# A two-layer graph transformer on one core: both layers and the first stretch in an order that a list schedule in the kernel plans

## The chip, the core and the metric

The kernel runs on one core of a Trainium2 chip. A core has TensorE (PE; matrix products into PSUM, with PEld its weight loads), VectorE (DVE), ScalarE (ACT), GpSimd (POOL, which here issues the indirect transfers) and SyncE (SP, which issues the plain ones), each with an instruction queue of its own that runs in order, and 16 DMA engines that they share. The metric is the device time of one execution in microseconds.

## What is computed

There are 6250 nodes with 128 features and a type out of 16, and 200,000 edges, sorted by destination, with a type out of 32. Two layers of this run one after the other (H = 8 heads of HS = 16):

```python
k = typed_linear(x, ntype, Wk).reshape(n, H, HS)      # q, v alike: one 128x128 matrix for each node type
kT = jnp.einsum('nhd,htdo->nhto', k, Watt)            # one 16x16 matrix for each head and edge type
vT = jnp.einsum('nhd,htdo->nhto', v, Wmsg)
kw, m = kT[src, :, etype], vT[src, :, etype]
a = jnp.einsum('ehd,ehd->eh', kw, q[dst]) * pri[:, etype].T / SQRT_D
att = edge_softmax(a, dst, n)
hag = jax.ops.segment_sum((m * att[:, :, None]).reshape(-1, H * HS), dst, num_segments=n)
h = jax.nn.silu(typed_linear(hag, ntype, Wa))
alpha = jax.nn.sigmoid(skip[ntype])[:, None]
h = layernorm(h * alpha + x * (1.0 - alpha)) * g + b
```

The result is `layernorm(x + (h @ ff_w + ff_b))`. All data are float32.

## The kernel before

**Table.** For a layer, a table in DRAM has 32 rows for each node, one for each edge type, with 128 values of kT and 128 of vT: 49 tiles of 128 nodes, 4 MiB a tile. An edge then needs one row of the table, and a tile of 128 destination nodes gets its s-th edges by one indirect gather of 128 rows (`gather`, L544). Nodes are ordered by in-degree, so that a tile has 61 to 23 such slots: 1613 gathers a layer.

**First stretch.** The edges' start positions are found by POOL's gathers and VectorE's comparisons (L218 to L256), nodes are ordered (L259 to L315; scatter of records at L309), slots are filled (`idx_all`, L329), types and x are brought into the new order (L360 to L395). Then (L519 to L531) for each group of four tiles `typed` builds k and v: for each of 16 node types VectorE masks the transposed rows (`xm`, L472) and TensorE adds a product for each of two weights (L476). For each tile `table_rows` makes 16 products of 32 rows by 512 columns (L503), four of which use the four row groups of TensorE; VectorE (L508) and ScalarE (L510) copy them from PSUM into one buffer `st` of 4 MiB, and four transfers of 1 MiB (L531) write it to the table. Each float32 product is two instructions in the profile.

**Layers.** For a layer, `free` issues gathers on POOL into a ring of 64 (layer 0) or 96 (layer 1) slots as slots come free. `attend` does a tile in pieces of up to 16 slots: q times k (L563), sum by head (L565), a softmax over the slots (L568 to L578), weights times v (L586), sum over slots (L590, L591). When a group of four tiles is done, `behind` works on it while the next group is attended: `finish` (typed products with Wa, SiLU, mix with x, norm), then in layer 0 `project_next` (typed products k, v, q, then the table rows of layer 1 tile by tile into `st`, copied by ScalarE alone, and one indirect scatter of 4 MiB a tile on POOL, L715), in layer 1 `head` (last product, norm, one indirect scatter of the output a tile, L738). Layer 0's queries are computed in `queries`, a group ahead.

**Order.** The parts that run beside `attend` are generators; `STEPS` and `REST` say how many of their steps are taken at each pause of `attend`. Engines' queues are in order, so a step written out early waits at its place and holds what is behind it.

Of the kernel before, what the change touches and what calls it, by code (L numbers as in the profile page):

```python
# [41 lines left out]
RINGS = (64, 96)  # L42
REST = 3
BINS = 64
NBLK = 512
GT = 4
FAR = float(1 << 21)
# [4 lines left out]
ROWT = True  # L52
STEPS = {("queries", 0): 9, ("queries", 1): 1, ("behind", False): 20, ("tile", False): 8,
         ("behind", True): 33, ("tile", True): 0}
# [18 lines left out]
def gnn_kernel(ctx: ExitStack, tc: tile.TileContext, x, src, dst, etype, ntype, Wk, Wq, Wv, Wa,  # L73
# [16 lines left out]
    GROUPS = [list(range(t, min(t + GT, NTILE))) for t in range(0, NTILE, GT)]  # L90
# [3 lines left out]
    assert max(profile) + 1 <= min(RINGS)  # L94
# [9 lines left out]
    qrows = dtile("qrows", [NP, P])  # L104
# [20 lines left out]
    for state in states:  # L125
        nc.sync.dma_start(
            out=state.rearrange("(t p) c -> p t c", p=P),
            in_=init[:, None, :].to_broadcast([P, NTILE, 2 * H + P]),
        )
# [14 lines left out]
    early = ctx.enter_context(ExitStack())  # L144
    tp = early.enter_context(tc.tile_pool(name="tp", bufs=1, side="right"))
# [33 lines left out]
    nc.sync.dma_start(out=csort_rows, in_=comb)  # L179
    with tc.tile_pool(name="prep_ps", bufs=1, space=bass.MemoryType.PSUM) as pps:  # L180
# [18 lines left out]
    ps = ctx.enter_context(tc.tile_pool(name="ps", bufs=1, space=bass.MemoryType.PSUM))  # L199
    wp = ctx.enter_context(tc.tile_pool(name="wp", bufs=1))  # L200
    ap = ctx.enter_context(tc.tile_pool(name="ap", bufs=2))
    masks = [ap]

    def bank(i):


        return ps.tile([P, GT * P], F32, tag=f"b{i}", name=f"b{i}")

    def load_typed(name, w, bufs=1):
        t = (wp if name == "wa" else tp).tile([P, NT, P], F32, tag=name, name=name, bufs=bufs)  # L210
        nc.sync.dma_start(out=t, in_=w.rearrange("t d o -> d t o"))
        return t


    pp = keep.enter_context(tc.tile_pool(name="prep2", bufs=1, side="right"))
    NC1 = NTILE + 1
    stage = ExitStack()
    sp = stage.enter_context(tc.tile_pool(name="search", bufs=2, side="right"))  # L218
    nid = pp.tile([P, NC1], F32, tag="nid")
    nc.gpsimd.iota(nid, pattern=[[1, NC1]], base=0, channel_multiplier=NTILE,  # L220
                   allow_small_or_imprecise_dtypes=True)
    ones_b = pp.tile([P, P], BF16, tag="ones_b")
    nc.vector.memset(ones_b, 1.0)
# [748 lines left out]
```

## Time and profile before

| | |
|---|---|
| median of 3 runs | 6803.65 us (6802.91 to 6808.02) |
| profiled execution | 6805.36 us, span 6803.6 us |
| mean granted TensorE clock | 0.639 |
| busy: PE, DVE, ACT, POOL | 2779.5, 3521.3, 913.1, 3561.3 us |
| DMA | 950.01 MB, mean 140 GB/s |

A busy share is an average over stages with different limits; the stages are told apart in the rows below. In the rows, `a <- b` names what is written and what is read; a bracket at the end of a row is the time for which the engine had stood idle, and what released it.

### The profile page before, as it was taken

Reading aid. Unit: us, or ns where it says so; the run is one execution under the profiler, and the core shown is the slowest. Engines: PE = TensorE matmul, PEld = TensorE weight load, DVE = VectorE, ACT = ScalarE, POOL = GpSimd, SP = SyncE. Lnnn points to the kernel's source line nnn. Section 1 sums busy time; section 2 is a strip of 40 time slices with the busy share of each in tenths; the row PEclk is TensorE's granted clock in tenths of the full one; section 3 lists DMA queues with packets and bytes.
Section 4 is the critical chain, followed back from the end, with each engine's and each line's share of the span. In section 5 each row is a group of like instructions: output and inputs, shape, how many; then the busy total and the mean of one; then the engine's idle time right before and its main releaser. Section 6 shows DMA issues by size and latency. Waiting matters only on the chain.

```text
span 6803.6 us, 31981 instructions
## 1 busy us (share of the span) xinstructions
PE 2779.5 (41%) x7380; PEld 1378.6 (20%) x7380; DVE 3521.3 (52%) x4748; ACT 913.1 (13%) x1713; POOL 3561.3 (52%) x3543
## 2 busy tenths in 40 slices
PE   1569999513353443644644666730110111111203
PEld 0124444201121221222222233320000000000001
DVE  5433433456566644644543644114665666567748
ACT  0123222100211111111111112220000000000001
POOL 4530000476767747436436431027777777777774
PEclk9657777656575665766766776755555555555556
DMA  6065655633545445344345333343333333333332
GB/s 165 12 238 242 253 218 216 208 104 93 179 137 192 141 141 173 109 155 148 124 159 168 129 137 136 124 165 100 106 103 101 106 108 107 106 104 106 106 105 61
DMA packets 335615, 950.01 MB, mean 140 GB/s; under 512 B 89712, under 2 KB 173164, under 8 KB 304056
## 3 DMA queue, kind: packets, MB, share of 16 engines
q0 software_dynamic: 171376, 645.92, 29.5%
q1 hardware_dynamic: 164040, 301.98, 12.5%
q14 instruction: 140, 1.15, 0.1%
q8 instruction: 59, 0.97, 0.1%
HBM read 514.82 MB, written 432.84 MB: 139 GB/s over the span
## 4 chain that ended last, share of the span: by engine, by line
issue 54%; POOL 16%; DVE 8%; DMA 3%; PE 0%; POOLq 0%; ACT 0%; DVEq 0%; SPq 0%; another core or an unknown queue 0%; ACTq 0%
POOL ring L544 15%; DVE add L590 2%; DMA ring<-table,idx_all 2%; DVE ring L586 2%; DVE xm L472 1%; DVE ring L563 1%; DVE b L565 1%; POOL table L715 0%; POOL out_dram L738 0%; PE b L476 0%; POOLq L544 0%; DMA table<-st,rec 0%; DVE den L576 0%; DMA bk<-in_L_gnn_Watt_dram 0%; DVE b L572 0%
## 5 line engine op out<-in xcount | busy, mean ns | idle before, releaser
L544 POOL DMA_INDIRECT ring<-table,idx_all x3226 | 3239.0, 1004 | 2409.3 <-issue 973.7
L563 DVE TENSOR_TENSOR ring<-ring,b 128x2048 f32<-128x2048 f32 (+13 forms) x269 | 469.6, 1749 | 1484.4 <-DMA ring<-table,idx_all 1459.3
L472 DVE SCALAR_TENSOR_TENSOR xm<-types,b 128x512 f32<-128x512 f32 (+1 forms) x1040 | 627.2, 651 | 1177.3 <-PE b L476 1090.2
L503 PE MATMUL b<-bv,vT 32*128 32x512 f32 x1568 | 740.4, 1023 | 1035.2 <-ACT st L510 975.3
L510 ACT COPY st<-b 128x512 f32<-128x512 f32 x1225 | 644.9, 593 | 1217.0 <-DMA table<-st,rec 802.4
L590 DVE TENSOR_REDUCE add<-ring 128x128 f32<-128x2048 f32 (+13 forms) x269 | 733.1, 2725 | 0.2
L503 PE MATMUL b<-bk,kT 32*128 32x512 f32 x1568 | 673.7, 987 | 119.5 <-ACT st L510 117.1
L503 PEld LDWEIGHTS b<-bv,vT 32*128 32x128 f32 x1568 | 313.2, 278 | 1276.6 <-ACT st L510 1131.5
L476 PE MATMUL b<-xm,wk 128*128 128x512 f32 (+1 forms) x832 | 456.0, 633 | 240.5 <-DVE xm L472 238.0
L463 PE MATMUL b<-ident,hag 128*128 128x128 f32 x98 | 28.8, 374 | 1259.2 <-DVE hag L835 1116.4
L476 PE MATMUL b<-xm,wq 128*128 128x512 f32 (+1 forms) x832 | 433.1, 644 | 159.9 <-DVE xm L472 145.9
L565 DVE TENSOR_REDUCE b<-ring 128x128 f32<-128x2048 f32 (+13 forms) x269 | 470.8, 1750 | 0.6
L586 DVE TENSOR_TENSOR ring<-ring,b 128x2048 f32<-128x2048 f32 (+13 forms) x269 | 462.9, 1744 | 0.0
L476 PE MATMUL b<-xm,wv 128*128 128x512 f32 (+1 forms) x832 | 441.4, 615 | 0.0
L508 DVE COPY st<-b 128x512 f32<-128x512 f32 x343 | 225.5, 688 | 412.6 <-DMA table<-st 207.9
L476 PE MATMUL b<-xm,wa 128*128 128x512 f32 (+1 forms) x832 | 398.0, 635 | 100.1 <-DVE xm L472 100.1
L503 PEld LDWEIGHTS b<-bk,kT 32*128 32x128 f32 x1568 | 292.7, 271 | 293.7 <-ACT st L510 215.1
L715 POOL DMA_INDIRECT table<-st,rec x49 | 49.1, 1003 | 557.0 <-ACT st L510 513.4
L573 ACT ACTIVATE b<-b 128x264 f32<-128x264 f32 (+21 forms) x98 | 37.4, 381 | 2027.1 <-DVE b L572 2010.7
L463 PEld LDWEIGHTS b<-ident,hag 128*128 128x128 f32 x98 | 15.0, 171 | 1278.0 <-DVE hag L835 1124.6
L476 PEld LDWEIGHTS b<-xm,wk 128*128 128x128 f32 x832 | 168.1, 212 | 445.5 <-DVE xm L472 270.8
L476 PEld LDWEIGHTS b<-xm,wq 128*128 128x128 f32 x832 | 176.1, 221 | 396.0 <-issue 200.5
(155 smaller groups left out, 1873.0 us busy)
## 6 DMA issues: line engine op xcount, KB each, us to landing
table<-st SPq DMA_DIRECT2D x196, 1024.0 KB
ring<-table,idx_all POOLq DMA_INDIRECT x3226, 2.8
types<-tyrow SPq DMA_DIRECT2D x36, 256.0 KB
state<-init SPq DMA_DIRECT2D x2, 3528.0 KB
state<-state SPq DMA_DIRECT2D x98, 72.0 KB
xs<-xperm SPq DMA_DIRECT2D x24, 256.0 KB
rows<-in_x_dram SPq DMA_DIRECT2D x12, 256.0 KB
types_i<-in_node_type_dram SPq DMA_DIRECT2D x12, 256.0 KB
```

Source lines behind the costliest of these rows:

```text
L463: nc.tensor.transpose(t_ps[:, j * P : (j + 1) * P], rows[:, j], ident)
L472: nc.vector.scalar_tensor_tensor(xm[:, i, :M], types[:, :M], float(t0 + i), xT[:, :M], op0=ALU.is_equal, op1=ALU.mult)
L476: nc.tensor.matmul(acc[c][:, :M], w[:, t0 + i], xm[:, i, :M], start=(t0 + i == 0), stop=(t0 + i == NT - 1))
L503: nc.tensor.matmul(tab, cT[c][rows, nodes], blk[rows, t0 : t0 + per].rearrange("p t o -> p (t o)"), start=True, stop=True)
L508: nc.vector.tensor_copy(to, tab.rearrange("p (t o) -> p t o", o=width))
L510: nc.scalar.copy(to, tab.rearrange("p (t o) -> p t o", o=width))
L544: nc.gpsimd.indirect_dma_start(out=rings[-1][:, place], out_offset=None, in_=tables[layer], in_offset=bass.IndirectOffsetOnAxis(ap=idx[:, ...
L563: nc.vector.tensor_tensor(kk, kk, q[:, None, :].to_broadcast([P, m, P]), op=ALU.mult)
L565: nc.vector.tensor_reduce(sc[:, s0 : s0 + m], kk.rearrange("p s (h d) -> p s h d", h=H), axis=AX.X, op=ALU.add)
L586: nc.vector.tensor_tensor(vv.rearrange("p s (h d) -> p s h d", h=H), vv.rearrange("p s (h d) -> p s h d", h=H), sc[:, s0 : s0 + m, :, None ...
L590: nc.vector.tensor_reduce(add, vv.rearrange("p s c -> p c s"), axis=AX.X, op=ALU.add)
L715: s = nc.gpsimd.indirect_dma_start(out=by_node, out_offset=bass.IndirectOffsetOnAxis(ap=rec[:, t0 + j, 2:3], axis=0), in_=st.rearrange("p ...
```

## The change

Nearly all of the kernel's body is written anew. What it does:

- Every part is a generator that yields what its next step needs: the engine (or two to choose from), an estimated duration, and times to wait for. `Plan.run` starts, again and again, the step that could start first by these estimates (`RANK` breaks ties) and so writes out the instructions in the order of that simulated time, inside `tc.manual_schedule()`. TensorE's steps are timed by `Clock`, whose rate goes between 1200 and 2400 columns a microsecond.
- First stretch: `prepare` (edges, order, slots) is one thread, `first_typed` and `first_tables` are others, beside it. Groups have two tiles; k and v are 256 columns wide each in one bank, and layer 0's q is computed here as well, as 128-wide products with the masked rows as weights, kept in `qall` and scattered to DRAM by position (`first_queries`). There are four banks for table products; either of ScalarE and VectorE copies them. `st` is freed by halves.
- Weights of layer 0 and the states' initial values are loaded ahead of the sort check; weights now come before the states.
- Layers: gathers, attention and what is behind are threads. `behind` holds a lock for its PSUM banks until the queries are copied, `next_tables` one for `st`. Table copies go to ScalarE or VectorE. A table scatter is placed `MARGIN` = 8 us after its planned readiness, an output scatter `LATE` = 40 us. The last groups have 3, 2, 2, 1 and 1 tiles. Rings are 64 and 96 slots, as before, allocated for each layer. q comes from DRAM in both layers and is copied into PSUM.

```diff
+MARGIN = 8.0
+RECS_US = 3.3
+XG_US = 2.4
+LATE = 40.0
+RANK = dict(table=0, empty=0, gather=1, attend=1, prepare=2, mask=3, typed=3, late=4, query=1)
+GATHER_US = 1.31
+HOP_US = 0.12
...
+    def run(self):
+        while self.threads:
+            best = None
+            for t in self.threads:
+                at = self.start(t)
+                if at is not None:
+                    key = (at[1], -1 if at[2] == "POOL" and t[0] != RANK["gather"] else t[0], t[1])
+                    if best is None or key < best[0]:
+                        best = (key, t, at)
+            _, t, (end, us, e) = best
+            if e == "PE":
+                self.free[e], end, state = self.clock.run(us, t[4][1])
+            else:
+                self.free[e] = end
+            end += HOP_US
+            self.step(t, (end, e) if isinstance(t[4][0], tuple) else end)
...
+    LAST, a = [], 0
+    for n in [GT] * ((NTILE - 9) // GT) + [GT - 1] * ((NTILE - 9) % GT // 3) + [3, 2, 2, 1, 1]:
+        LAST.append(list(range(a, a + n)))
+        a += n
...
+        plan.spawn(mask(), RANK["mask"])
+        for t in range(NT):
+            busy[t].us = yield "PE", Work(M * (len(cols) + len(rows))), [ready[t], clear]
+            xm = masks.pop(t)
+            todo = [(w, acc[:, :M], None) for w, acc in cols]
+            todo += [(w, acc[:, c : c + P], slice(c, c + P)) for w, acc in rows for c in range(0, M, P)]
+            for i, (w, to, c) in enumerate(todo):
+                last_of = t == NT - 1 and i in ends
+                if c is None:
+                    nc.tensor.matmul(to, w[:, t], xm, start=False, stop=last_of)
+                else:
+                    nc.tensor.matmul(to, xm[:, c], w[:, t], start=False, stop=last_of)
...
+                    us = yield "PE", Work(TAB, width / P), [*needs, *emptied[-len(banks):][:1]]
+                    tab = banks[len(emptied) % len(banks)]
+                    nc.tensor.matmul(tab, cT[rows, nodes], blk[rows, t0 : t0 + per].rearrange("p t o -> p (t o)"),
+                                     start=True, stop=True)
+                    def empty(to=st[:, t0 : t0 + per, c0 : c0 + width], tab=tab, done=done, us=us, i=i):
+                        done.us, e = yield ("ACT", "DVE"), (act_us(TAB), dve_us(TAB)), [us, free[i]]
+                        (nc.scalar.copy if e == "ACT" else nc.vector.tensor_copy)(
+                            to, tab.rearrange("p (t o) -> p t o", o=width))
...
+    def send(dest, c, filled, done):
+        us = yield "SP", 0.8, filled
+        for s0 in (c * RT // 2, c * RT // 2 + RT // 4):
+            nc.sync.dma_start(out=dest[:, s0 : s0 + RT // 4], in_=st[:, s0 : s0 + RT // 4])
+        done.us = (yield "DMA", 5.4, [us]) + 2.0
...
+    def first_queries():
+        for i, g in enumerate(GROUPS):
+            for t in g:
+                yield "POOL", GATHER_US, [placed, queried[i]]
+                s = nc.gpsimd.indirect_dma_start(
+                    out=qrows[0], out_offset=bass.IndirectOffsetOnAxis(ap=posn[:, t : t + 1], axis=0),
+                    in_=qall[:, t], in_offset=None, bounds_check=NP - 1, oob_is_err=False)
...
+    with tc.manual_schedule():
+        plan.spawn(first_typed(), RANK["typed"])
+        plan.spawn(first_tables(), RANK["table"])
+        plan.spawn(prepare(), RANK["prepare"])
+        plan.spawn(first_queries(), RANK["late"])
+        plan.run()
...
+    def next_tables(i, kT, vT, bk, bv, us, at):
+        turn = locks["s"].take()
+        for j, t in enumerate(LAST[i]):
+            halves = yield from table_rows(tabs, at["rows"], kT, vT, j, bk, bv, [us, turn], [at["st"]] * 2)
+            us = yield "SP", 0.0, halves[0] + halves[1]
+            us = yield "POOL", GATHER_US, [us + (MARGIN if i + 2 < NG else 0.0)]
+            s = nc.gpsimd.indirect_dma_start(
+                out=by_node, out_offset=bass.IndirectOffsetOnAxis(ap=rec[:, t, 2:3], axis=0),
+                in_=at["rows"].rearrange("p t c -> p (t c)"), in_offset=None, bounds_check=NP - 1, oob_is_err=False)
+            at["st"] = us + 16.0
+        locks["s"].give(us - MARGIN)
...
+    def gathers(layer, ring, size, landed, freed):
+        for s in range(SLOTS):
+            us = yield "POOL", GATHER_US, [freed[s - size]] if s >= size else []
+            gather(layer, ring, idx_all, s, s % size)
+            landed[s].us = us + 2.5
...
+            with tc.manual_schedule():
+                plan.spawn(gathers(layer, ring, size, landed, freed), RANK["gather"])
+                plan.spawn(attends(fp, layer, ring, cut(size), st, weights, wa, landed, freed), RANK["attend"])
+                plan.run()
```

## Rows read from the trace of the kernel before

**Rows 1.** Windows by stage: the stretch (us from the span's start), its length, busy time and (number of instructions) of PE, PEld, DVE, ACT and POOL, mean granted TensorE clock, DMA share, GB/s.
```profile
0.00:359.00 359.00, 110.64 (x410) 46.43 (x410) 164.95 (x286) 22.05 (x40) 185.91 (x181) 0.83 0.35 87
359.00:1239.00 880.00, 772.17 (x2269) 368.94 (x2269) 344.48 (x523) 249.47 (x461) 38.59 (x39) 0.74 0.60 243
...
4115.60:4538.50 422.90, 283.56 (x845) 164.52 (x845) 81.56 (x177) 119.05 (x230) 12.64 (x14) 0.69 0.38 148
1252.00:4538.50 3286.50, 1600.60 (x3958) 814.46 (x3958) 1617.97 (x2097) 526.00 (x1012) 1666.39 (x1663) 0.66 0.43 143
4538.50:6722.00 2183.50, 266.71 (x656) 132.02 (x656) 1328.95 (x1700) 102.87 (x178) 1660.38 (x1652) 0.55 0.36 105
6722.00:6803.60 81.60, 29.41 (x87) 16.76 (x87) 64.76 (x142) 12.68 (x23) 10.04 (x10) 0.65 0.06 19
```

**Rows 2.** Who reads and writes the tables: line, engine, operation, tiles and count; duration in ns (least, median, most); first and last start in us.
```profile
L544 POOL DMA_INDIRECT ring<-table,idx_all x3226: 995/1002/1686, 1252.0 to 6722.1; - x190
L531 SPq DMA_DIRECT2D table<-st x196: 319/423/2391, 359.2 to 1238.9; - x196
L715 POOL DMA_INDIRECT table<-st,rec x49: 962/1017/1018, 1754.2 to 4521.8; - x49
```

**Rows 3.** POOL's timeline around the first table scatter of layer 0: start, duration, line, operation, count, idle time before it and its releaser. Between the second and third row no other scatter is issued; the rows left out are gathers.
```profile
1754.19 1.02 POOL L715 DMA_INDIRECT table<-st,rec  x1 [0.31 <-issue]
...
1763.38 1.00 POOL L544 DMA_INDIRECT ring<-table,idx_all  x1 [0.30 <-issue]
1767.96 1.00 POOL L544 DMA_INDIRECT ring<-table,idx_all  x1 [3.58 <-DMA table<-st,rec]
```

**Rows 4.** POOL's waits: what waited for what, us in total, times, longest. The first three rows are of layer 0 (1252 to 4538.5), the fourth of 2040 to 4115, the fifth of 1250 to 2040.
```profile
POOL table L715 <- ACT st L510: 513.4, 20, 87.4
...
POOL ring L544 <- DVE add L590: 463.4, 19, 53.9
POOL ring L544 <- DMA table<-st,rec: 80.9, 22, 5.4
...
POOL table L715 <- ACT st L510: 154.0, 9, 21.5
...
POOL ring L544 <- DVE add L590: 56.4, 7, 19.1
```

**Rows 5.** Timeline of the first stretch's preparation: SP's issue of the states' initial values, the first transposes, the first gather of the edge search, the first x gather, and the copy into `st` that waited longest.
```profile
3.08 11.50 SPq L126 DMA_DIRECT2D state<-init  x2
...
72.94 1.09 PE L463 MATMUL b<-ident,rows 128*128 128x128 f32 x4
...
74.23 1.19 POOL L247 DMA_INDIRECT part<-dsort,blk_i  x1 [4.71 <-DVE blk_i L241]
...
345.58 1.00 POOL L392 DMA_INDIRECT xg<-in_x_dram,rec  x1 [0.30 <-issue]
...
370.73 1.29 DVE L508 COPY st<-b 128x512 f32<-128x512 f32 x2 [57.80 <-DMA table<-st]
```

**Rows 6.** One group of four tiles in the table stage: windows of its typed products (706 to 731) and of its table rows (731 to 775), then rows of its timeline (`x2`, `x8`: that many instructions).
```profile
706.00:731.00 25.00, 25.00 (x59) 10.92 (x59) 8.14 (x13) 0.00 (x0) 0.00 (x0) 0.99 0.13 51
731.00:775.00 44.00, 34.95 (x135) 17.20 (x133) 18.14 (x28) 20.53 (x38) 0.00 (x0) 0.80 0.81 334
...
731.94 1.14 PE L503 MATMUL b<-bk,kT 32*128 32x512 f32 x8
...
743.46 1.56 ACT L510 COPY st<-b 128x512 f32<-128x512 f32 x3 [4.12 <-DMA table<-st]
```

**Rows 7.** TensorE and ScalarE on layer 0's last tile, one tile wide: 128-wide typed products, then a single table product (two instructions) and the transpose behind it, with the copy of that transpose's operand.
```profile
4505.21 0.39 PE L476 MATMUL b<-xm,wk 128*128 128x128 f32 x2
4505.43 0.39 PE L476 MATMUL b<-xm,wv 128*128 128x128 f32 x2
...
4509.99 1.12 PE L503 MATMUL b<-bk,kT 32*128 32x512 f32 x2
4510.10 0.27 ACT L516 COPY qT<-b 128x128 f32<-128x128 f32 x1
4511.04 0.33 PE L606 MATMUL b<-ident,qT 128*128 128x128 f32 x1
```

**Rows 8.** Groups of instructions by line over the span: busy us, mean ns, idle before and releasers.
```profile
L510 ACT COPY st<-b 128x512 f32<-128x512 f32 x1225 | 644.9, 593 | 1217.0 <-DMA table<-st,rec 802.4 <-PE b L503 240.4 <-DMA table<-st 173.2
L472 DVE SCALAR_TENSOR_TENSOR xm<-types,b 128x512 f32<-128x512 f32 (+1 forms) x1040 | 627.2, 651 | 1177.3 <-PE b L476 1090.2 <-PE b L463 86.9
L508 DVE COPY st<-b 128x512 f32<-128x512 f32 x343 | 225.5, 688 | 412.6 <-DMA table<-st 207.9 <-PE b L503 204.5
```

**Rows 9.** Timeline behind layer 0's last gather: table scatters and the copies between them, the steps of `finish` from its copied product to the next typed product, the last scatter and layer 1's first gather.
```profile
4138.09 0.99 POOL L715 DMA_INDIRECT table<-st,rec  x1 [21.47 <-ACT st L510]
4149.98 2.05 ACT L510 COPY st<-b 128x512 f32<-128x512 f32 x4 [12.17 <-DMA table<-st,rec]
...
4204.78 0.59 ACT L516 COPY vT<-b 128x512 f32<-128x512 f32 x1 [15.36 <-PE b L476]
...
4216.54 2.47 DVE L472 SCALAR_TENSOR_TENSOR xm<-types,b 128x512 f32<-128x512 f32 x4
...
4521.75 0.97 POOL L715 DMA_INDIRECT table<-st,rec  x1 [35.10 <-ACTq L613]
...
4538.50 1.05 POOL L544 DMA_INDIRECT ring<-table,idx_all  x1 [15.78 <-issue]
```

More of the change, by code (lines that the diff above doesn't have):

```diff
@@ L46 @@
 GT = 4
+GL = 2
 FAR = float(1 << 21)
@@ L197, in gnn_kernel, with run @@
     prep.close()
[L199 to L211, printed above, removed]
-        return t
+    def run(steps):
+        try:
+            at = steps.send(None)
+            while True:
+                at = steps.send((0.0, at[0][0]) if isinstance(at[0], tuple) else 0.0)
+        except StopIteration as end:
+            return end.value
@@ new lines, in gnn_kernel, with apart @@
+    on_pool = [None]
+    def apart(s, group):
+        kept = [on_pool[0]] if on_pool[0] is not None else []
+        tc.declare_no_dep(s.ins, group=group, keep=kept, reason="every node has rows of its own")
+        tc.add_to_no_dep_group(group, s.ins)
+        on_pool[0] = s.ins
+    wk, wv, wq, bk, bv = w0
+    st = first.tile([P, RT, ROW], F32, tag="st", name="st")
+    made = [When() for _ in GROUPS]
+    used = [When() for _ in GROUPS]
+    columns = [None] * len(GROUPS)
+    HALF = GL * P
@@ L544, in gather @@
+    def gather(layer, ring, idx, s, place):
         nc.gpsimd.indirect_dma_start(
-            out=rings[-1][:, place], out_offset=None, in_=tables[layer],
+            out=ring[:, place], out_offset=None, in_=tables[layer],
             in_offset=bass.IndirectOffsetOnAxis(ap=idx[:, s : s + 1], axis=0),
@@ L777, in cut, with queries @@
+    def queries(rows, j, t, read, to, ready):
+        us = yield "ACT", act_us(P), [rows[1], read]
+        q = sb[:, QC:] if (profile[t] + 1) * H <= QC else ak[:, :P]
+        nc.scalar.copy(q, rows[0][:, j])
+        to[t] = q
+        ready.us = us
     def cut(size):
-        out = []
+        pieces = []
         for t in range(NTILE):
@@ L833, in gnn_kernel @@
+                _, den = yield from attend(ring, pieces[t], pen_all[:, span], profile[t], qs[t],
+                                           states[layer][t * P : (t + 1) * P], hag[:, j], landed[span], free, [ready[t]],
+                                           read[t])
+                past[t].us = plan.free["DVE"]
+                us = yield "DVE", 0.4 + dve_us(P), ()
                 nc.vector.tensor_scalar(den, den, 1e-30, None, op0=ALU.max)
```

1124 lines of the change are left out of this document (667 added, 457 removed).

## The prediction

> **What bounds the kernel now.** I read the windows by stage first, then POOL's waits, then single places of the timeline. [rows 1] cut the span of 6803.6 us at the first and last gather of each layer [rows 2]: a first stretch of 1252 us, layer 0 from 1252 to 4538.5, layer 1 from there to the end. The profiled run took 6805.4 us, its span 6803.6, the median of the runs is 6803.65: the sum below is of spans and stands for the median as it is.
>
> Layer 1 is bound by POOL. A gather starts every 1.31 us ((1763.38 - 1754.19) / 7) [rows 3], and 1613 gathers with 45 output scatters at that price are 2172 us; the stage took 2183.5 from first to last gather [rows 1]. Nothing but the 81.6 us behind the last gather can still be won there.
>
> Layer 0 issues 1613 gathers and 49 table scatters, 1662 x 1.31 = 2177 us, and takes 3286.5. The difference of 1110 us is POOL standing still, and the waits say for what [rows 4]: 513 us a table scatter waited for ScalarE's copies into st, of which 154 lie among the gathers and the rest behind the last one; 463 us a gather waited until VectorE freed ring slots; 81 us a gather waited until a table scatter had landed; some 50 us are small. No engine is full: VectorE is busy 1618 of 3286 us, TensorE 1601 [rows 1]. So layer 0 is a matter of order: VectorE and TensorE come to the projection in lumps, and POOL's queue holds scatters that are not ready.
>
> The first stretch has two parts that barely overlap. In 359 us the edges are sorted into slots, POOL going from step to step [rows 5], and the first table rows leave only then: a copy into st waited 57.8 us for the first transfer [rows 5]. Then 880 us of table, in turns: for four tiles, 30 us of typed products with TensorE full at a clock of 0.99 of 2.4 GHz and DMA at 0.13, then 44 us of table rows with DMA at 0.81 and 334 GB/s, where the copies wait for transfers [rows 6].
>
> **The change, part by part: first stretch.** It removes the turns (typed products and table rows are interleaved), hides the preparation, and adds layer 0's queries here. Per tile of 128 nodes, at the full clock: a 512-wide product is two instructions of 25.00 / 59 = 0.42 us, 0.85 [rows 6], so k and v for 256 columns cost 16 x 2 x 0.43 / 2 = 6.9 us a tile (half the columns, two tiles). The queries use 128-wide products at 0.22 us each [rows 7]: 16 x 0.22 = 3.6. A batch of four 32-row table products runs side by side, eight instructions in 1.14 us [rows 6]; a lone one holds TensorE as long, 1.05 us until the next instruction starts, whose operand was copied by 4510.4 [rows 7]. Sixteen products are then 4.6 us in full batches, 16.8 us one by one. Transposes 0.3. That is 15.4 to 27.6 us. I take 16.4, near the lower end: there are four banks, ScalarE and VectorE empty one in 0.59 and 0.69 us [rows 8], so some three or four are free whenever a typed step of 1.3 us is over.
> Transfers do not bind: 196 writes of 1 MiB [rows 2] are 205 MB, at 334 / 0.81 = 412 GB/s 499 us, and all DMA of the first 359 us is 0.35 of them, 126 us [rows 1]; together 625 of some 800.
> POOL's preparation takes 272 us from 74 to the first x gather at 346 [rows 5]: 148 instructions of 1.31 are 194, 78 are gaps. With the x gathers and the new query scatters it is 246 instructions, 322 us, and ends near 74 + 78 + 322 = 474; at twice the price an instruction, if transfers are late beside the table's, near 796. Both lie before the table's end, so I cost it at nothing; without that cover it is the 272 us again.
> The first transposes start at 73 us now; SP's state writes, 11.5 us of issue, are put ahead of them [rows 5], so I start at 85. Then 49 x 16.4 = 804, 16 us for the last transfer and the first gather: 905, where 1252 is now. Bounds: 15.4 gives 856. At the clock of 0.74 that the table stage has on average [rows 1] 16.4 becomes 22.2 and the stretch 1189; I take the full clock, because it stood at 0.99 where TensorE was kept full [rows 6] and here it hardly pauses.
>
> **Layer 0.** The list schedule moves work between queues but leaves POOL's 2177 us. What is left of the waits:
> - Table scatters: the eighth POOL transfer behind one waits until it has landed, 3.58 us [rows 3]. It showed 22 times only [rows 4], since POOL stood for other reasons at the rest. With a stream that does not stop it comes 49 times: 175 us. This is a part of today's time that the change uncovers. Bounds 81 to 175.
> - Ring: 56.4 us in the first 790 us of the layer [rows 4], where the tiles have 61 to 37 of 64 slots and little else runs. The ring is not changed, so I keep 60; bounds 0 (a plan that frees in time) and 150 (a third of today's 463).
> - Scatters that wait for st: 154 among the gathers today [rows 4]. The scatter is now placed 8 us behind its planned readiness; I take 45, bounds 0 and 154: nearer to none, since a tile's chain (30 us, below) is shorter than its gathers.
> - Behind the last gather: 423 us today [rows 1], because the last five tiles' projection runs alone, with 87 us of typed products [rows 4] and 22.4 a tile of table rows [rows 9]. The last groups are now of 3, 2, 2, 1, 1 tiles, and for one tile the chain is landing 3, attention 13 (half of the 1329 / 49 = 27 us that VectorE spends on a tile in layer 1 [rows 1], as the rest comes before the last landing), typed products 4 + 11 (48 x 0.22), the norm between them 12 (4204.8 to 4216.5) [rows 9], table copies on two engines 7, scatter to first gather 17 (4521.75 to 4538.50) [rows 9]: 67. The group ahead holds the same lock for up to one such chain without landing and scatter: 110 taken, bounds 67 and 150.
> Cover: a tile's own table chain is 11 us of copies on ScalarE alone, 1 of issue, 11.4 of transfer, 22.4 [rows 9], with the 8 us margin 30; the last tiles' gathers take 24 x 1.31 + 5 = 36 us. TensorE needs four maps of 16 products at 0.22, 14 us, and 5 for tables; at half the clock 38. VectorE has 1618 us today, loses the query masks (208 x 0.65 = 135) and gains up to half of 784 table copies (270): 1753. All below 2567, but TensorE at half clock would just fail at the end.
> Sum 2177 + 175 + 60 + 45 + 110 = 2567.
>
> **Layer 1.** 2183.5 stays; the output scatters are put 40 us late so that they do not hold gathers. Behind the last gather a single tile: 3 + 13 + 4 + 12 and 8 for the head = 40, and 15 for the tile ahead of it: 55. Together 2238.
> Total 905 + 2567 + 2238 = 5710 us, a ratio of 0.839.
>
> **The rivals.**
> A. TensorE pays for the mixing. If table products come alone between full-height ones, a tile costs 27.6 us and the first stretch 85 + 1352 + 16 = 1453: the total is 6258. For it speaks the 1.05 us of the lone product [rows 7]; against it, four banks that come free by themselves. The Trainium skill, TensorEngine Tiling (Array Packing), Key Properties, says that a change of tiling mode drains TensorE. The 1.05 us row agrees in kind; by the rule each of 16 turns a tile would pay it.
> B. Layer 0's order does not come out on the chip: POOL's 1110 us stay, of whatever names. 905 + 3286 + 2238 = 6429. The lumps would have to survive a plan that models each engine.
> C. The other side. POOL's queue is in order, and a scatter placed too early holds every gather behind it, and they hold VectorE. If TensorE lags behind the plan, each group's first scatter waits for the typed products, 87 us, and each other one 21.5, as behind the last gather today [rows 4, 9]: 15 x 87 + 34 x 21.5 = 2036 us, and 7746 in all. It decides from (6817 - 5710) / 49 = 22.6 us a scatter on. Against it: chains of 30 us under 36 to 60 us of gathers, and a late group is not early again for the next.
> D. The landing waits vanish too, since plan or ring stalls absorb them, and the order holds: 5710 - 175 - 60 - 45 = 5430.
>
> **How the numbers follow.** Forecast case 0.64, D 0.16, A 0.09 (partly, between 5900 and 6258), B 0.07, C 0.04 (half of it above 6817). The prediction is 5710. The range goes down to D's 5430 and up to 6050, where the clock of the first stretch lies at its average today (5710 + 284 = 5994) or scatters and ring take their upper bounds (5710 + 109 + 90 + 40 = 5949); beyond it lie B, C and half of A, and a little below D. A difference of 0.2%, 14 us, is about what a measurement of this kernel can tell. Faster: all but half of C and a trace of no effect, 0.97; same 0.01; slower 0.02.
>
> **What would show it.** First gather near 905, with TensorE above 0.9 busy at a clock above 0.9 in the stretch, and DMA busy without pauses. Between layer 0's first and last gather POOL's starts 1.31 us apart, one wait of some 3.6 us per scatter, few waits for the ring, and under 150 us from the last gather to layer 1's first. Layer 1 as long as now. The prediction is wrong if POOL's table scatters wait for copies by more than 10 us each, if the first stretch is above 1050, or if the 3.6 us waits are not there.

## The result, and the profile after

The kernel takes 5805.53 us (median of 4 runs, 5801.05 to 5807.33), the kernel before 6804.18 us in the same comparison: a ratio of 0.8531 (95% interval 0.8516 to 0.8545), 999 us less. The forecast was 5710 us with a range of 5430 to 6050; the time lies inside it, 95 us above the forecast. The profiled execution took 5804.55 us, its span 5802.8.

Windows by stage of the changed kernel, cut at the first and the last gather of each layer (columns as in [rows 1]):

```profile
0.00:1001.30 1001.30, 901.51 (x5063) 608.33 (x5065) 489.81 (x983) 298.74 (x575) 260.95 (x268) 0.98 0.68 249
1001.30:3313.50 2312.20, 1277.07 (x2900) 543.43 (x2900) 1555.77 (x1855) 409.09 (x794) 1653.71 (x1653) 0.66 0.53 174
3313.50:3585.50 272.00, 216.72 (x784) 133.31 (x784) 112.31 (x242) 75.56 (x141) 9.75 (x11) 0.68 0.35 146
3585.50:5751.00 2165.50, 269.77 (x652) 135.65 (x652) 1461.07 (x1804) 115.70 (x241) 1660.18 (x1658) 0.54 0.36 107
5751.00:5802.80 51.80, 17.95 (x73) 15.11 (x73) 28.50 (x84) 9.11 (x18) 4.85 (x5) 0.53 0.04 11
```

Beside the terms of the forecast (before: from [rows 1]; the difference is measured less forecast):

| stage | before | forecast | measured | difference |
|---|---|---|---|---|
| up to the first gather | 1252 | 905 | 1001.3 | +96 |
| layer 0, first to last gather (forecast 2177 + 175 + 60 + 45) | 2863.6 | 2457 | 2312.2 | -145 |
| behind its last gather | 422.9 | 110 | 272.0 | +162 |
| layer 1, first to last gather | 2183.5 | 2183.5 | 2165.5 | -18 |
| behind its last gather | 81.6 | 55 | 51.8 | -3 |

So the sum of layer 0 was right within 17 us (2567 against 2584) by luck: two errors of some 150 us cancel. The miss that is left is the first stretch. Of the gain, 551 us lie among layer 0's gathers, 251 in the first stretch and 151 behind layer 0's last gather.

POOL's waits in layer 0 (columns as in [rows 4]); the first three rows are from its first to its last gather, the others behind the last:

```profile
POOL ring L833 <- DMA table<-st,rec: 145.4, 39, 4.7
POOL ring L833 <- DVE add L885: 14.4, 4, 13.5
POOL table L1049 <- ACT st L451: 2.4, 2, 1.3
...
POOL table L1049 <- ACT st L451: 198.3, 7, 38.3
POOL table L1049 <- DVE xm L937: 24.7, 1, 24.7
POOL table L1049 <- ACTq L896: 23.5, 1, 23.5
```

Against [rows 4]: the ring went from 463 to 14 us, table scatters among the gathers from 154 to 2.4. POOL does nothing but issue, apart from 39 waits of 3.73 us and some 23 us of smaller ones. The scatters that still wait are the nine behind the last gather. No run undid the order of layer 0 alone, so how much of the 551 us is the plan's, and how much comes from table copies on two engines or from queries that are ready beforehand, was not separated.

TensorE's timeline in the first stretch (columns as in [rows 6]): a typed step is k, v and two query products, L412 and L414; table products are L442, two instructions each.

```profile
601.84 1.13 PE L442 MATMUL tab<-bk,kT 32*128 32x512 f32 x6
602.90 0.70 PE L412 MATMUL kv<-xm,wk 128*128 128x256 f32 x2
603.44 0.59 PE L412 MATMUL kv<-xm,wv 128*128 128x256 f32 x2
603.87 0.61 PE L414 MATMUL aq<-wq,xm 128*128 128x128 f32 x4
604.41 1.12 PE L442 MATMUL tab<-bk,kT 32*128 32x512 f32 x2
605.46 0.70 PE L412 MATMUL kv<-xm,wk 128*128 128x256 f32 x2
...
606.87 0.60 PE L412 MATMUL kv<-xm,wk 128*128 128x256 f32 x2
...
608.18 0.60 PE L412 MATMUL kv<-xm,wk 128*128 128x256 f32 x2
...
609.58 1.14 PE L442 MATMUL tab<-bv,vT 32*128 32x512 f32 x8
610.65 0.70 PE L412 MATMUL kv<-xm,wk 128*128 128x256 f32 x2
```

A typed step alone takes 1.31 us (606.87 to 608.18). With a run of table products before it the steps are 2.56 apart (602.90 to 605.46), and it is the same whether the run has one product (x2), three (x6) or four (x8): 1.25 us a run. TensorE has no pause here, and the mean granted clock of the stretch is 0.98 of 2.4 GHz, so a run that holds fewer than four products takes the time of a full one.

### The profile page after: what moved, and what is told of

Its sections match the earlier page's. It is cut to its first block, busy times and chain, and to the rows that moved or that the text cites. A ratio compares the mean times of both kernels' runs of the same rounds, so it can differ in the third digit from the quotient of the medians.

```text
span 5802.8 us, 36552 instructions
## 1 busy us (share of the span) xinstructions
PE 2683.0 (46%) x9472; PEld 1435.8 (25%) x9474; DVE 3647.5 (63%) x4965; ACT 908.2 (16%) x1768; POOL 3589.4 (62%) x3592
## 5 line engine op out<-in xcount | busy, mean ns | idle before, releaser
L833 POOL DMA_INDIRECT ring<-table,idx_all x3226 | 3229.8, 1001 | 1179.2 <-issue 997.3
L854 DVE TENSOR_TENSOR ring<-ring,sb 128x2048 f32<-128x2048 f32 (+13 forms) x261 | 453.8, 1739 | 889.9 <-DMA ring<-table,idx_all 877.3
L451 ACT COPY st<-tab 128x512 f32<-128x512 f32 x1165 | 628.1, 590 | 1198.6 <-PE tab L442 863.9
L885 DVE TENSOR_REDUCE add<-ring 128x128 f32<-128x2048 f32 (+13 forms) x269 | 735.5, 2734 | 9.1
L442 PE MATMUL tab<-bk,kT 32*128 32x512 f32 x1568 | 587.4, 784 | 330.9 <-ACT st L451 265.4
L442 PE MATMUL tab<-bv,vT 32*128 32x512 f32 x1568 | 577.4, 819 | 61.6 <-DVE st L451 34.2
L937 DVE SCALAR_TENSOR_TENSOR xm<-types,xb 128x512 f32<-128x512 f32 (+3 forms) x720 | 391.2, 584 | 241.8 <-PE aq L945 210.9
L945 PE MATMUL aq<-xm,wa 128*128 128x512 f32 (+3 forms) x960 | 448.0, 629 | 177.8 <-DVE xm L937 177.8
L856 DVE TENSOR_REDUCE sb<-ring 128x128 f32<-128x2048 f32 (+13 forms) x269 | 473.5, 1760 | 9.2
L881 DVE TENSOR_TENSOR ring<-ring,sb 128x2048 f32<-128x2048 f32 (+13 forms) x269 | 469.4, 1745 | 0.0
L451 DVE COPY st<-tab 128x512 f32<-128x512 f32 x403 | 266.9, 686 | 218.7 <-PE tab L442 164.2
L442 PEld LDWEIGHTS tab<-bk,kT 32*128 32x128 f32 x1568 | 183.4, 218 | 490.0 <-ACT st L451 359.5
L945 PE MATMUL ak<-xm,wk 128*128 128x512 f32 (+3 forms) x480 | 243.0, 591 | 107.2 <-DVE xm L937 107.1
L412 PE MATMUL kv<-xm,wk 128*128 128x256 f32 (+1 forms) x800 | 262.7, 410 | 9.2 <-DVE xm L397 9.2
L442 PEld LDWEIGHTS tab<-bv,vT 32*128 32x128 f32 x1568 | 193.5, 227 | 258.6 <-ACT st L451 162.5
L414 PEld LDWEIGHTS aq<-wq,xm 128*128 128x128 f32 x1568 | 238.7, 193 | 20.6
```

What stands on the lines that cost most here:

```text
L412: nc.tensor.matmul(to, w[:, t], xm, start=False, stop=last_of)
L414: nc.tensor.matmul(to, xm[:, c], w[:, t], start=False, stop=last_of)
L442: nc.tensor.matmul(tab, cT[rows, nodes], blk[rows, t0 : t0 + per].rearrange("p t o -> p (t o)"), start=True, stop=True)
L451: (nc.scalar.copy if e == "ACT" else nc.vector.tensor_copy)(to, tab.rearrange("p (t o) -> p t o", o=width))
L833: nc.gpsimd.indirect_dma_start(out=ring[:, place], out_offset=None, in_=tables[layer], in_offset=bass.IndirectOffsetOnAxis(ap=idx[:, s : s ...
L854: nc.vector.tensor_tensor(kk, kk, q[:, None, :].to_broadcast([P, m, P]), op=ALU.mult)
```

## The experiments

The first four ran beside runs of the kernel before at 6808.44 us.

**Runs of table products: fours, and finer steps.**

```diff
-                for g in range(P // width):
-                    us = yield "PE", Work(TAB, width / P), [*needs, *emptied[-len(banks):][:1]]
+                per_step = P // width if len(banks) == 4 else 1
+                for g0 in range(0, P // width, per_step):
+                    us = yield "PE", Work(TAB, width / P if per_step == 1 else 1.0), [
+                        *needs, *(emptied[-4:] if per_step == 4 else emptied[-len(banks):][:1])]
...
```

> First stretch only: the four 32-row table products of one half of k or of v become one step of TensorE's order, which waits until all four banks are empty, so that no batch goes out partly filled. In the order of the changed kernel the 784 table products of the first stretch stand in 257 runs (66 of one product, 12 of two, 71 of three, 104 of four, four long ones); here they stand as 196 fours. Theory (a run between full-height products costs TensorE 1.25 us whether it holds one product or four): some 74 runs fewer, 74 x 1.25 = 92 us, so the first gather starts near 910 instead of 1001 and the total is near 5713. Rival 1 (a product costs its quarter of a batch, 0.29 us, wherever it stands, and the 96 us by which the stretch was longer than forecast are lost to the preparation or to transfers): no change, within 15 us of 5805. Rival 2 (waiting for all four banks leaves TensorE idle): longer, by up to a copy of 0.6 us for each of 196 fours, 118 us, 5920.

```diff
-            busy[t].us = yield "PE", Work(M * (len(cols) + len(rows))), [ready[t], clear]
+            yield "PE", Work(M), [ready[t], clear]
...
+                if 0 < i <= len(cols):
+                    us = yield "PE", Work(M), ()
...
+            busy[t].us = us
```

> First stretch only, the opposite edit: a typed step of TensorE (k, v and two query products, 1.31 us) is cut into three steps of its order, so table products go between them as soon as a bank is empty. Same instructions, but the 784 table products now stand in 357 runs (168 of one, 28 of two, 111 of three, 46 of four) instead of 257. Theory (1.25 us a run): 100 x 1.25 = 125 us more, first gather near 1126, total near 5930. Rival 1 (a product costs 0.29 us wherever it stands): no change or, as banks are refilled sooner, a little shorter.

Finer steps: 5959.07 us (5955.15 to 5967.8), 154 more than the changed kernel where 125 were expected; the first gather starts at 1144.9. TensorE's windows of the table stage (from the first to the last table write) of the changed kernel, of the finer one, and of the fours:

```profile
111.00:992.70 881.70, 860.31 (x4678) 574.09 (x4679) 439.76 (x887) 293.27 (x566) 242.68 (x243) 0.98 0.68 259
```
```profile
122.20:1136.40 1014.20, 992.29 (x4683) 586.21 (x4683) 414.63 (x849) 319.59 (x600) 228.87 (x232) 0.96 0.59 224
```
```profile
109.50:976.60 867.10, 807.24 (x4688) 569.53 (x4686) 480.23 (x950) 259.30 (x504) 247.90 (x244) 0.94 0.69 264
```

The instructions are the same in number; 100 more runs make 132 us more of busy TensorE, 1.3 us a run. Rival 1 falls. The fours take 53 us of busy time away where 92 were expected. Part of the rest went to the clock, which is 0.94 in that stage instead of 0.98: busy time times clock is 843 us in the changed kernel, 759 with the fours and 953 with the finer steps, so by this estimate a batch of up to four products (270, 196 and 365 of them) costs some 1.1 us of full clock, with the fours and with the finer steps alike. In all, 5799.21 us (5790.79 to 5806.14) is no gain that can be told, and the first gather starts at 985.4, not 910. Where nothing is in the way, two tiles take 31.5 us (500.35 to 531.89), 15.8 a tile, as the theory has it; but TensorE stood idle for 60 us instead of 21 (rival 2, in part), of which 24 are one wait:

```profile
484.57 3.05 PE L445 MATMUL tab<-bv,vT 32*128 32x512 f32 x8 [24.12 <-ACT st L454]
```
```profile
478.99 0.20 DVE L614 CAST deg_p<-rec 128x49 f32<-128x49 int32 x1 [23.90 <-DMA rec<-recs]
```

The second row names the cause: VectorE stood before the copy of the sorted records, and the masks and table copies behind it in its queue stood too. So a second thing was just below the first: the preparation is planned with prices that are too low (`RECS_US` = 3.3; 49 scatters of records took 218 us in the changed kernel, some 4.5 each, since each waits there for the one before it to land).

**The preparation written out first.**

```diff
+        plan.spawn(prepare(), RANK["prepare"])
+        plan.run()
+        for e in plan.free:
+            plan.free[e] = max(plan.free.values())
         plan.spawn(first_typed(), RANK["typed"])
         plan.spawn(first_tables(), RANK["table"])
-        plan.spawn(prepare(), RANK["prepare"])
         plan.spawn(first_queries(), RANK["late"])
         plan.run()
```

> Undoes one part: the preparation (edge search, order, x gathers, slots) is written out to its end before the first typed products and tables, instead of beside them. The prediction costed the preparation at nothing because the table hides it. If that is right, and it also costs the table nothing, the first transposes start when TensorE's last product of the preparation is done, near 74 + 78 gaps + 246 - 49 instructions of POOL at 1.31 = 410 to 480 us instead of some 90, and the table stage keeps its 18.0 us a tile: first gather 1320 to 1390, total 6125 to 6195. Rival (the preparation slows the table stage and is where the missing 96 us went): the table stage falls to some 16.4 us a tile, first gather 1225 to 1295, total 6030 to 6100.

6167.76 us (6165.23 to 6169.35); the first gather starts at 1352.1, 351 us later. The preparation is hidden, as costed. It is not free: without it the table stage takes 844.7 us instead of 881.7, so the rival holds for 37 us of the 96. TensorE is then idle for 5 us of the stage instead of 21, and busy 21 us less, at a clock of 0.99:

```profile
499.00:1343.70 844.70, 839.39 (x4655) 562.09 (x4653) 364.41 (x742) 265.40 (x507) 45.70 (x47) 0.99 0.63 252
```

**The last groups.**

```diff
-    for n in [GT] * ((NTILE - 9) // GT) + [GT - 1] * ((NTILE - 9) % GT // 3) + [3, 2, 2, 1, 1]:
-        LAST.append(list(range(a, a + n)))
-        a += n
+    LAST = [list(range(a, min(a + GT, NTILE))) for a in range(0, NTILE, GT)]
```

> Undoes one part: the last groups are of four tiles and a single one again, instead of 3, 2, 2, 1, 1. In the changed kernel 272 us pass between layer 0's last gather and layer 1's first, and nine table scatters fall into them, 24 to 39 us apart. Theory 1 (the one buffer st sets the pace: landing 12 us, then copies, 30 us a tile, and the tables of the last nine tiles are all still to be done whatever the groups): layer 0 gets longer by the one tile for which tile 40 waits longer, some 40 us, and layer 1's end by the longer last chain, less than 20; total 5830 to 5865. Theory 2 (the prediction's: the chain of the last groups sets it): the stretch goes back towards the 423 us of the kernel before, total near 5950.

5849.74 us (5848.83 to 5858.68), 44 more. Behind layer 0's last gather 313.9 us pass instead of 272, and nine scatters lie there as before. Theory 1 stands: the small last groups are worth 42 us, and the rest of the stretch is nine tiles at some 30 us each.

**Margin, prices, halves.** These four ran on a chip on which the kernel before takes 7187.94 us. Since the changed kernel was not beside them, they are read by stage and against each other; the totals that were expected, for a chip on which it takes 6805, can't be tested there.

```diff
-MARGIN = 8.0
+MARGIN = 0.0
```

> The changed kernel, with table scatters of layer 0 placed in POOL's queue at the moment the plan holds them for ready (margin 0) instead of 8 us later. In the changed kernel 41 scatters among the gathers waited 17 us in all. Theory (the plan's times are right to some few us, so the 8 us are a cushion that is rarely used): each of some 40 scatters waits 2 to 4 us and holds the gathers behind it, 80 to 160 us more; total 5885 to 5965. Rival 1 (the prediction's case C, TensorE and the copies lag behind the plan by tens of us): 20 us and more a scatter, above 6600. Rival 2 (the plan is late rather than early, the cushion is idle): within 15 us of 5805.

Margin 0: 6639.75 us (6632.69 to 6655.87); layer 0 takes 3015 us, 82 more than with margin 8 in the next kernel (2933), whose layers are those of the changed kernel; the scatters among the gathers wait 388 us in 29 waits against 267 in 25. That is 13 us a wait, under the 22.6 a scatter from which case C would have decided. The 82 us lie at the lower end of what the theory said, and rival 2 (an idle cushion) falls there. On the first chip margin 0 was not tried. (The 41 scatters and 17 us of the expectation take in the first scatter behind the last gather, which waited 14 us; the forty among the gathers waited 2.4.)

The next edit is shown against the fours.

```diff
-RECS_US = 3.3
-XG_US = 2.4
+RECS_US = 4.5
+XG_US = 4.0
...
-                    us = yield "PE", Work(TAB, width / P if per_step == 1 else 1.0), [
+                    us = yield "PE", Work(TAB, width / P) if per_step == 1 else Work(690), [
```

> The fours of the earlier experiment, with three planned prices set to what the traces show: a scatter of records 4.5 us instead of 3.3 (49 took 218 us in the changed kernel), an x gather 4.0 instead of 2.4 (49 took 196 us), a four 1.15 us of TensorE. With fours alone the table stage went at 15.8 us a tile where nothing stood in its way, but VectorE stood 24 us before the copy of the sorted records, SyncE 30 us before the same transfer, and 106 us before x gathers, with table writes behind them. Theory (a part of the preparation written out too early now holds the table): these waits go, first gather at 940 to 960 instead of 985, total 5755 to 5775. Rival (the writes or the copies are the next bound just below, whatever the order): first gather stays within 10 us of 985.

Fours with prices: 6513.53 us (6507.18 to 6516.42); the first gather starts at 1010.0, where the two kernels beside it that have the first stretch of the changed kernel start theirs at 1062 and 1065. In the last kernel below, on a chip like the first, it starts at 958.6, in the stretch that was expected (940 to 960) and 27 us before that of the fours alone. The waits named are nearly gone. SyncE's for x gathers, with the fours alone and in the last kernel:

```profile
SPq L635 <- DMA xg<-in_x_dram,rec: 106.3, 12, 14.8
```
```profile
SPq L637 <- DMA xg<-in_x_dram,rec: 9.7, 2, 9.3
```

Its wait for the sorted records went from 30 to 8 us. Which of the three prices did it was not separated, and one was misread: x gathers start 1.31 us apart, mostly in fours, and the 196 us are long because the query scatters that stand between them wait for the landing of earlier ones (101 us in 27 waits in the changed kernel).

```diff
+            def half_done(c, filled, i=i, t=t, done=at["st"]):
+                plan.spawn(place(i, t, c, at["rows"], filled, done[c]), RANK["table"])
...
+            out=by_half, out_offset=bass.IndirectOffsetOnAxis(ap=half_of[c][:, t : t + 1], axis=0),
+            in_=rows[:, c * RT // 2 : (c + 1) * RT // 2].rearrange("p t c -> p (t c)"), in_offset=None,
...
```

> The changed kernel, with each table scatter of layer 0 made as two of 2 MiB, one for each half of st, each placed when its own half is copied; the copies of a half wait for that half alone. 49 more POOL instructions. Theory, two parts. (1) The 3.7 us waits are for a 4 MiB scatter that has not landed when the eighth transfer behind it comes, 8 x 1.31 = 10.4 us later; a half lands in some 7 us, so the 39 waits (145 us) go and 40 x 1.31 = 52 us of issue come: the stretch of gathers goes from 2312 to near 2220. (2) Behind the last gather the buffer sets the pace, 30 us a tile of which 12 us pass between a scatter and the first copy behind it; with halves some 20 us a tile, nine tiles, 272 to near 180 us. Together 5620. Rival to (1): both halves are issued close together, the second lands as late as the whole did, and the waits stay: no gain there, 5715. Rival to (2): typed products and norms of the last groups set the pace, the stretch stays within 20 us of 272.

> The fours with their prices and the halves together. If the first stretch and layer 0 are separate stages, the gains add: 5805 - 45 - 185 = 5575 (5680 if the 3.7 us waits stay). If they share something, less than the sum.

Halves: 6581.11 us (6575.79 to 6625.76); with fours and prices 6529.98 (6516.35 to 6555.8), 51 less, of which the first gather, at 1015.8 instead of 1062.1, has 46. With halves that is still 16 us more than the fours with prices alone take. The halves and the changed kernel were then run side by side, on a chip where the kernel before takes 7166.96 us, so again not the 6805 for which the totals were expected.

> The changed kernel itself, as a yardstick for the two kernels beside it, since the last four ran on a chip on which the kernel before took 7188 us. If the kernel before takes some 6805 us here, this takes 5805 within 10 us.

> The halves again, against the changed kernel on one chip. On the last chip the 3.7 us waits had gone (7 us in 2 waits instead of 145 in 39) and the stretch behind the last gather was 214 us instead of 271, so the tail part is expected to repeat: -57 us. Of the gathers' stretch (2312 us) the theory says -145 + 52 = -93 where POOL sets the pace; total 5805 - 150 = 5655. Rival: where scatters wait for copies as they did on the last chip (558 us in 54 waits against 463 in 32), the gathers' stretch gets longer by 30 to 80 us, and the total stays near 5805.

> Fours with their prices, and halves. The first gather came 47 to 55 us earlier with fours and prices on the last chip (1010 and 1016 against 1062 and 1065). If the stages are separate, this is the halves' time less 50 us: 5605, or 5755 by the rival above.

The changed kernel 6504.49 us (6499.86 to 6517.22; ratio 0.9086, 0.9069 to 0.9103), the halves 6563.9 (6546.52 to 6575.3), all together 6514.28 (6484.52 to 6539.68). POOL's waits from layer 0's first to its last gather, of the changed kernel there (2606 us) and of the halves (2716 us):

```profile
POOL table L1049 <- ACT st L451: 228.9, 25, 26.1
POOL ring L833 <- DMA table<-st,rec: 148.3, 40, 4.7
POOL ring L833 <- DVE add L885: 59.2, 5, 24.2
```
```profile
POOL table L1063 <- ACT st L451: 374.3, 44, 33.8
POOL ring L838 <- DVE add L890: 123.6, 10, 24.2
```

The 3.7 us waits are gone, so they were for the landing of 4 MiB. But scatters wait 145 us more for copies and gathers 64 more for the ring: the gathers' stretch grew by 110 us, and in all the halves cost 59 us here. That is the rival, by more than the 30 to 80 us it named. All together takes 50 us less than the halves, as expected, and so no less than the changed kernel. The stretch behind the last gather went from 276 to 220 us. Whether halves among the gathers pay on a chip where POOL sets the pace was not tried.

**What held on both chips, in one kernel.** Fours with their prices; halves for the last five groups alone.

```diff
+            late = i >= NG - 5
...
+                                           half_done if late else None)
```

> Fours with their prices, and scatters in halves for the last nine tiles alone; the other forty tiles keep one scatter of 4 MiB. What worked on either chip, without the 40 extra POOL instructions among the gathers. If the stages are separate: the first gather 45 to 55 us earlier, the gathers' stretch of layer 0 as in the changed kernel, the stretch behind the last gather 57 us shorter. On a chip where the kernel before takes 6805 us: 5805 - 50 - 57 = 5700; where it takes 7170: 6505 - 107 = 6400, a ratio of 0.893 instead of 0.9086. Rival: what is gained in the first stretch is lost in layer 0, as the 7 us between the total of the fours with their prices and that of the changed kernel's ratio on the slower chip suggest: 5750 or 6450.

5723.85 us (5719.77 to 5727.16), a ratio of 0.8407 (0.8396 to 0.8419) to the kernel before at 6806.42: 82 us below the changed kernel, 24 above what was expected. Its stages, the table writes, layer 0's gathers, the stretch behind them, and layer 1:

```profile
110.30:950.20 839.90, 798.66 (x4689) 562.56 (x4687) 490.77 (x967) 251.00 (x489) 246.28 (x244) 0.95 0.71 273
958.60:3272.10 2313.50, 1280.86 (x2928) 547.42 (x2928) 1559.63 (x1873) 412.15 (x800) 1654.50 (x1652) 0.67 0.54 174
3272.10:3506.80 234.70, 197.94 (x756) 116.75 (x756) 103.67 (x220) 75.44 (x139) 18.42 (x20) 0.77 0.41 169
3506.80:5725.30 2218.50, 284.48 (x725) 147.60 (x725) 1488.13 (x1887) 124.66 (x259) 1666.76 (x1662) 0.55 0.36 105
```

The first gather comes 43 us earlier, the stretch behind layer 0's last one is 37 us shorter, where 57 were expected, and the rest is unchanged: the stages add, the rival falls. Of the 92 us that fewer runs should give, about half came; TensorE is busy 62 us less, but idle 41 us instead of 21, and its mean clock is 0.95 instead of 0.98.

## Why the prediction was right, and where it was not

**First stretch, +96: the term "4.6 for tables in full batches, about 1 more" was mis-sized.** The typed products came out as costed: 392 steps of 1.31 are 514 us, 10.5 a tile. The step that failed is "some three or four are free whenever a typed step of 1.3 us is over". In the order that the plan wrote, 784 table products stand in 257 runs, 66 of them with a single product; with the long runs counted by fours that is 270 batches x 1.25 = 337 us instead of 49 x 5.6 = 274, +63. The preparation beside the table costs 37, which I had put at nothing; 16 of them are idle time of TensorE. Two of the marks named beforehand hold: the first gather is below 1050, and TensorE is 0.98 busy at a clock of 0.98 in the table stage. The third does not: DMA, which was to be busy without pauses, has a share of 0.68. The stretch starts 12 us earlier than taken (transposes at 73), and 29 us pass from the last typed product at 972 to the first gather, with the last table products among them, where I had 16. Rival A was thus right in kind and small in size: I had priced a lone product at 1.05 us [rows 7], but the plan, which prices it as a quarter of a batch, sends only 66 alone. Of the 1.25 us of a run, 0.85 is what one 512-wide product takes at this clock [rows 6]; four products side by side take no longer, and 0.40 come on top. The Trainium skill (TensorEngine Tiling (Array Packing), Key Properties) says that a change of tiling mode drains TensorE. The 0.40 us agree with it in kind; no run measures a drain by itself.

**Layer 0 up to its last gather, -145: right in kind, waits over-sized.** POOL's starts are 1.31 us apart, and the landing waits, uncovered by a stream that does not stop, came as forecast: 145 us in 39 waits of 3.73, where I had 49 of 3.58. All 49 was wrong, because nine scatters fall behind the last gather. That it is the eighth transfer behind a scatter that waits is the program's doing and not shown to be the chip's: in the trace POOL's transfers take turns with eight completion semaphores, and the gather that waits is the next user of the scatter's. The ring cost 14 us instead of 60 and late scatters 2.4 instead of 45. That a plan which models each engine frees and fills in time is how I read this; the plan and the margin were not separated on this chip.

**Behind layer 0's last gather, +162: the chain was costed for the last tile, and it is the pace of nine.** I had 67 us for one tile's chain and 43 for the group ahead under the same lock, and named less than 150 us as a mark. The scatters:

```profile
3328.48 1.01 POOL L1049 DMA_INDIRECT table<-st,rec  x1 [13.99 <-ACT st L451]
3365.06 0.99 POOL L1049 DMA_INDIRECT table<-st,rec  x1 [35.56 <-ACT st L451]
3393.35 0.96 POOL L1049 DMA_INDIRECT table<-st,rec  x1 [27.31 <-ACT st L451]
...
3544.33 0.96 POOL L1049 DMA_INDIRECT table<-st,rec  x1 [32.40 <-ACT st L451]
3568.75 0.96 POOL L1049 DMA_INDIRECT table<-st,rec  x1 [23.46 <-ACTq L896]
3585.49 1.05 POOL L833 DMA_INDIRECT ring<-table,idx_all  x1 [15.77 <-issue]
```

Nine tiles, all of the last five groups, (3568.75 - 3328.48) / 8 = 30.0 us apart. They wait 27 us each, more than the 10 us that the prediction named as a sign of being wrong, while the forty among the gathers hardly wait. Each tile's copies wait for one buffer `st`:

```profile
3340.42 1.07 ACT L451 COPY st<-tab 128x512 f32<-128x512 f32 x2 [12.22 <-DMA table<-st,rec]
3376.96 1.07 ACT L451 COPY st<-tab 128x512 f32<-128x512 f32 x2 [12.18 <-DMA table<-st,rec]
```

From a scatter to the first copy behind it 12 us pass, then come 18 us of products and copies. I knew this chain as 30 us and took it as covered by 36 us of gathers a tile. The step that failed is the number of tiles: the prediction says that the last five tiles' projection runs alone, and then costs one tile and a group ahead. In the kernel before, thirteen table scatters lay behind the last gather (first row, L715 alone; [rows 4] has 20 waits for copies, 9 of them among the gathers). In the changed kernel POOL issues 324 gathers before the first table scatter (second row, L833 alone), more than the 309 slots of the first seven tiles (61, 45, 43, 41, 40, 40, 39).

```profile
4115.60:4538.40 422.80, 12.64 (x13) 0.69 0.38 148
```
```profile
1001.30:1437.40 436.10, 324.22 (x324) 0.57 0.40 115
```

So the tables are seven tiles behind the gathers from the first one on and nine at the end, and behind the last gather nothing covers them. What sets this distance was not tried. Halves shortened the pace (eighteen scatters, 17 intervals in 217 us, 25.5 a tile) and the stretch to 235 us; smaller groups alone gave 42. What sets the 25.5 that are left was not separated: half a scatter's landing, products and typed steps all lie in it. The Trainium skill (DMA: Bandwidth & Descriptors, Anatomy of one DMA — SWDGE (gpsimd) path) gives 2.0 us and 436 bytes a ns for a transfer, 11.6 us for 4 MiB as an estimate; the 12 us agree.

**Layer 1, -21.** It takes 2165.5 us from first to last gather instead of the 2183.5 of before. That the late output scatters did it is not shown: in the kernel before they waited for nothing either (0.3 us each; forty of them in this stretch, not 45). What has gone are gathers' waits for VectorE, 23 us. POOL's waits in layer 1 of the kernel before:

```profile
POOL ring L544 <- DVE add L590: 13.4, 5, 5.5
POOL out_dram L738 <- issue: 10.1, 33, 0.3
POOL ring L544 <- DVE den L833: 9.4, 4, 5.2
```

Behind the last gather 51.8 us pass, where 55 were forecast.

**The rivals.** B (the order does not come out) and C (scatters too early) did not come: 40 scatters among the gathers waited 2.4 us together. On the slower chip C came in part, 229 us in 25 waits at margin 8. D was half right: ring and late scatters vanished, the landing waits did not.

## What to carry to other kernels

When a few small products are put between large ones of another shape, count the runs in the order as written, and price a run, not a product: wait until a run is full, and expect less than the sum, since other waits lie just below. A queue that never stops uncovers the waits of its own earlier transfers, and work that is hidden under it is hidden only up to its last instruction: what is still to be done then runs at its own pace, so count how many tiles lie between the two, which the trace of before already shows. A price in a plan that is too low puts a wait into a queue that something else needs.

## What the runs showed of the hardware that was not expected

The same two kernels differ by 5% and 12% between two chips: 6804 and 7167 us before, 5806 and 6504 us after. In the other comparisons the kernel before took 6806 and 6808 us, and on a third chip 7188. Instructions take as long (a piece's sum over slots 2734 ns on both), POOL's issues too. But layer 0's gathers take 2606 us instead of 2312 and layer 1 2562 instead of 2217. What the trace shows there is that one engine often starts late after another, and that the profile names no instruction that ended the wait (`remote`); how much of the difference this makes was not added up. VectorE's masks on the slower chip, behind TensorE's products, and then the masks on the other:

```profile
1351.60 4.45 PE L945 MATMUL aq<-xm,wa 128*128 128x512 f32 x10
1359.34 0.69 DVE L937 SCALAR_TENSOR_TENSOR xm<-types,xb 128x512 f32<-128x512 f32 x1 [4.91 <-remote]
1364.94 0.69 DVE L937 SCALAR_TENSOR_TENSOR xm<-types,xb 128x512 f32<-128x512 f32 x1 [4.91 <-remote]
1370.54 0.69 DVE L937 SCALAR_TENSOR_TENSOR xm<-types,xb 128x512 f32<-128x512 f32 x1 [4.91 <-remote]
1375.44 0.69 DVE L937 SCALAR_TENSOR_TENSOR xm<-types,xb 128x512 f32<-128x512 f32 x1 [4.21 <-remote]
```
```profile
1298.84 0.69 DVE L937 SCALAR_TENSOR_TENSOR xm<-types,xb 128x512 f32<-128x512 f32 x1 [1.02 <-PE aq L945]
1300.81 0.69 DVE L937 SCALAR_TENSOR_TENSOR xm<-types,xb 128x512 f32<-128x512 f32 x1 [0.17 <-PE aq L945]
```

The products in the first row end at 1356.05, and the mask behind them starts 3.3 us later; on the other chip a mask starts some 0.03 us after the end of the product that releases it. The late starts stand 5.60, 5.60 and 4.90 us apart, all multiples of 0.70. The cause stays open: each of the slower chips was used at one time only, so it is not shown either that it is the chip and not something beside the kernel. The change is worth less there, 0.909 instead of 0.853.
